# A two-layer mixture-of-experts kernel: head re-ordered, second gate moved to VectorE, five tiles brought home by one-hot products

## The chip, the cores and the metric

The kernel runs on one core of a Trainium2 chip, in one launch. The metric is the time of an execution on the device in microseconds (us). The engines are named as the profile names them: PE is TensorE, DVE is VectorE, ACT is ScalarE, POOL is GpSimd, and SP is SyncE, which here only issues transfers.

## The reference

The input x has 8 sequences of 256 rows (tokens) of 128 numbers, 2048 tokens in all. Two layers each add something to x. Everything is float32.

```python
# layer 0: conditioning by attention pooling, per sequence
scores = einsum('bsa,a->bs', tanh(x @ W1 + b1), v)
mask   = l <= j, l >= j or l != j, by the sequence's prompt type (0, 1, 2)
pooled = softmax(where(mask, scores, -1e30)) @ x / count(mask)
# layer 0: 8 experts, all computed, with gates from the logits
logits = pooled @ gate_weight.T
gates  = logits * (logits >= the 3072nd smallest of all 16384 logits)
x = x + sum_e gates[e] * (gelu_tanh(pooled @ w1[e].T + b1[e]) @ w2[e].T + b2[e])
# layer 1: an adapter chosen by the sequence's language, then a layer norm
h  = relu(x @ W1[lang] + b1[lang]) @ W2[lang] + b2[lang]
xc = layernorm(x + h) * gamma[lang] + beta[lang]
# layer 1: 8 experts, the two best per token
xn = layernorm(xc) * gamma + beta
w, idx = top_2(softmax(xn @ gate_w)), w normalised to sum 1
x = x + xc + sum over the 2 of w * (gelu(xn @ w1[e] + b1[e]) @ w2[e] + b2[e])
```

## The kernel before

The 2048 tokens are 16 blocks of 128, and these form four groups of four blocks. A list UNITS (L30) cuts the groups into five units: units 0 to 2 are whole groups of 512 tokens ("full units"), units 3 and 4 are halves of the last group with 256 tokens each.

**The head (L122 to L502)** runs as it is written, on PE, DVE, ACT and POOL. The tokens (xp, one tile per group) arrive on SP's and ACT's queues; all columns (col: weights with 32 or 8 columns, biases, gamma and beta) come by POOL's queue (L129), and after them the prompt types ptb (L130). Behind the tokens SP issues bva (the bias and v), the languages lgi, eight loads of the rows again in another layout (xg, L139), the sixteen loads of layer 0's weights (L144 and L147), and the loads that depend on the languages (L190 to L204). PE turns the tokens (turned_tokens, L238), forms the pooling's inner products (products, L247, "units" in the profile) and the gate's products (gate_logits, L260, "g0p"), both with columns of col; ACT takes the tanh (bent, L254); PE makes the scores (L281). DVE makes flags from the prompt types (own and out8, L312 to L318) and, in places (L321), the counts cnt of the tokens under the mask. Then come running maxima (scans, L347 and L349), their transposes by PE (tops, L365), the exponentials on ACT, and the pooling products with xg (L390).

**Layer 0's experts (layer, L895)** are PE's main work: for each unit and each expert four products hp_first (L945) and four yp_first (L925) of 512 columns, or of 256 in half units. ACT evicts hp_first with gelu (L947). DVE multiplies yp_first by a row of gates, gbc_first, and adds it up (accumulate, L901, with L913 and L915). SP loads gbc_first from DRAM into four buffers ahead of use (L905).

**Work beside it.** What else PE, DVE and POOL have to do in this stretch is written as generators. After each product call (in half units: after each second one) pump (L880) takes one step, up to the next `yield`, of the generator that stands first in the queue `behind`. So a number of yields between two steps is a number of product calls between two groups of PE instructions. PE's instructions have this order; a scheduler places those of the other engines. The first generators are the poolings of later groups and the threshold search (threshold, L521): DVE counts with an accumulating operation (L531) how many logits lie below trial values. When a unit's last expert is added up, its generator adapt (L689) is queued:

- It adds the tokens (L694), transposes the sum (fp, L566), projects down (adp, L704 to L707: one product for each of two sequences, 256 columns each, with two relu operations on DVE into ha) and up (dp, L711 to L716).
- The first layer norm (normed, L569: statistics on DVE, a power on POOL at L582, and a scaling by block at L587), gamma and beta of the language (L728 and L729), the second layer norm, whose result zr is also what is scattered.
- The second gate. After CHAIN_GAP = 5 yields PE transposes the normalised rows (znp, L749), DVE applies gamma and beta (znT, L754), PE multiplies by the gate's columns in four column groups (l1q, L763), DVE copies (l1s, L766), PE transposes back (l1p, L770), and DVE copies the logits (lg, L778). Half units use a shorter way without l1q (L775).
- DVE picks the two best experts (top_one, L597, twice) and forms running counts (sofar, L802). After two yields PE sums these over the tokens (kp, L808 and L809). From kp come the places in DRAM, and POOL scatters each block's rows, one indirect transfer per block and choice (L830), into xs, sorted by expert.
- After units 2, 3 and 4 (SLOTS, L32) DVE lists which tiles of 128 rows are complete (listed, L656).

**Layer 1's experts** work on 36 tiles of 128 rows (SURE, L46; three more behind a condition at L1184 are not needed with these inputs). Tile k is fetched with its weights by SP (L983 and L993), turned (xtp, L1019), and goes through hidden (hps, L1034, and gelu on ACT, L1036) and output (yps, L1043, and yt on DVE, L1047). hidden takes the expert's second bias from b2all (L1031), a copy of all eight rows on all partitions, loaded early (L629). POOL scatters the tile's rows yt into ys (L1050), two rows for each token. From tile PLACED = SURE − 4 = 32 on there is no scatter: DVE makes a 0/1 matrix by token (home, L1089), and PE multiplies it with yt (brought, L1103, "late" at L1106).

**The ending (L1160 to L1191)** runs as it is written on all engines. SP loads the two rows of each token back in eight pieces (yg; n counts sequences): n = 0 to FIRST − 1 after the scatter of tile 28, FIRST to 5 after that of tile 30 (L1055 to L1060), 6 and 7 at the start of the ending (L1164). DVE adds them (add, L1074: two operations), SP stores. For n = 6 and 7 the sums of late are added as well (L1182) and stored last. Of the four groups of late products, one stands before the last yps and three behind it.

## Time and profile before

| What | us |
|---|---|
| Median of 4 runs | 346.49 (345.98 to 347.41) |
| Profiled execution, its own time | 346.3 |
| Span of the profiled execution | 344.6 |
| Busy: PE | 335.5 |
| Busy: DVE | 197.3 |
| Busy: ACT | 170.6 |
| Busy: POOL | 93.5 |
| First hp_first (L945) starts at | 23.4 |
| First xtp (L1019) starts at | 260.5 |
| Last yps (L1043) starts at | 335.8 |

The profile shows one execution from its first to its last instruction, and its times count from the start of that span. The mean granted clock of PE was 0.998. A line of a timeline begins with a start and a duration in us and names the engine, the line of the kernel, the operation, what it writes and reads, and how many instructions it sums up; in brackets stands how long its engine was idle before it and what ended that. PE's instructions overlap, so that their cost is read from one start to the next. A product in float32 shows as two instructions. Groups give the busy time, the mean duration in ns, and the idle time before them.

### The profile page before, as it was taken

The numbers are of one execution on the slowest core, as the hardware profiler recorded it, in microseconds if no ns is written. First come the engines' busy times: TensorE is split into PE (matmuls) and PEld (weight loads), VectorE is DVE, ScalarE is ACT, GpSimd is POOL, SyncE is SP. The second block draws the span as 40 slices with busy tenths as digits, with TensorE's granted clock in tenths as the row PEclk, the third lists the DMA queues.
The fourth block names the chain that finished last, engine by engine and source line by source line (L and its number), as shares of the span: only waits on it lengthen the run. The fifth ranks groups of instructions, "written<-read, shape, count | busy, mean of one in ns | idle before, by whom it ended". The sixth has DMA issues, their size and how long they took to land. (4 is left out here: it accounts for less than half of the span.)

```text
span 344.6 us, 6117 instructions
## 1 busy us (share of the span) xinstructions
PE 335.5 (97%) x1662; PEld 221.2 (64%) x1662; DVE 197.3 (57%) x835; ACT 170.6 (50%) x393; POOL 93.5 (27%) x146
## 2 busy tenths in 40 slices
PE   7999999999999999999999999999999999999994
PEld 6795444444444444444444468877887999999993
DVE  2884766642235584757361247569768668733474
ACT  3476345543444333323543334644456777777660
POOL 6600000000000031174017001206604465765530
PEclk9999999999999999999999999999999999999999
DMA  6893599955214300121212010112376675587565
GB/s 179 252 342 74 143 345 384 380 191 145 76 56 141 80 30 30 30 86 39 62 38 62 23 30 30 42 35 73 81 204 166 169 205 171 156 218 217 147 208 178
DMA packets 35771, 47.56 MB, mean 138 GB/s; under 512 B 5449, under 2 KB 18588, under 8 KB 35736
## 3 DMA queue, kind: packets, MB, share of 16 engines
q1 hardware_dynamic: 32744, 42.17, 41.1%
q0 software_dynamic: 2144, 4.19, 3.6%
q10 hardware_dynamic: 848, 0.79, 0.7%
q8 instruction: 15, 0.25, 0.3%
q14 instruction: 20, 0.16, 0.2%
HBM read 32.66 MB, written 14.66 MB: 137 GB/s over the span
## 5 line engine op out<-in xcount | busy, mean ns | idle before, releaser
L947 ACT ACTIVATE hT_first<-hp_first,col 128x512 f32<-128x512 f32 (+1 forms) x160 | 93.2, 601 | 91.5 <-PE hp_first L945 90.4
L925 PE MATMUL yp_first<-hT_first,w 128*128 128x512 f32 (+1 forms) x320 | 120.1, 512 | 0.0
L945 PE MATMUL hp_first<-poolT,w 128*128 128x512 f32 (+1 forms) x320 | 119.8, 512 | 0.0
L925 PEld LDWEIGHTS yp_first<-hT_first,w 128*128 128x128 f32 x320 | 58.6, 190 | 45.3 <-issue 41.0
L945 PEld LDWEIGHTS hp_first<-poolT,w 128*128 128x128 f32 x320 | 58.7, 190 | 44.5 <-issue 39.7
L830 POOL DMA_INDIRECT xs<-zr,pos x32 | 32.5, 1015 | 67.6 <-DVE holding L653 33.0
L1036 ACT ACTIVATE hs<-hps,col 128x128 f32<-128x128 f32 x144 | 40.7, 375 | 11.8 <-PE hps L1034 8.3
L913 DVE SCALAR_TENSOR_TENSOR part_first<-yp_first,col,gbc_first 128x512 f32<-128x512 f32 (+1 forms) x28 | 17.2, 615 | 39.6 <-PE yp_first L925 39.1
L1043 PE MATMUL yps<-w,hs 128*128 x288 | 38.3, 277 | 0.5 <-issue 0.2
L1050 POOL DMA_INDIRECT ys<-yt,xt x32 | 31.9, 996 | 24.5 <-DVE yt L1047 14.9
L1034 PE MATMUL hps<-xc,wt 128*128 128x128 f32 x288 | 38.2, 276 | 0.0
L1043 PEld LDWEIGHTS yps<-w,hs 128*128 128x128 f32 x288 | 35.0, 192 | 1.1 <-issue 0.9
L1034 PEld LDWEIGHTS hps<-xc,wt 128*128 128x128 f32 x288 | 35.1, 192 | 0.4 <-issue 0.2
L582 POOL TENSOR_TENSOR rstd_l<-ve_l,nhalf 128x4 f32<-128x4 f32 (+1 forms) x5 | 5.0, 1005 | 69.4 <-DVE ve_l L580 69.3
L1047 DVE SCALAR_TENSOR_TENSOR yt<-yps,xt,b 128x128 f32<-128x128 f32 x36 | 12.5, 348 | 18.1 <-PE yps L1043 18.0
L915 DVE TENSOR_TENSOR acc_first<-acc_first,part_first 128x512 f32<-128x512 f32 (+1 forms) x35 | 20.1, 580 | 0.5
L1021 ACT ACTIVATE xc<-xtp,col 128x128 f32<-128x128 f32 x36 | 16.7, 470 | 7.1 <-PE xtp L1019 7.0
L516 POOL DMA_DIRECT2D gd_L<-gT_L x1 | 0.7, 660 | 61.1 <-DVE gT_L L514 61.1
L933 ACT ACTIVATE y_first<-yp_first,col 128x512 f32<-128x512 f32 x8 | 5.5, 687 | 23.2 <-PE yp_first L925 14.6
L1031 DVE TENSOR_TENSOR b<-b2all,xt 128x128 f32<-128x128 f32 x36 | 10.4, 289 | 8.0 <-DVE yt L1047 3.8
L531 DVE TENSOR_SCALAR_CACHE_REDUCE fl<-logit,tr 128x128 bf16<-128x128 f32 x46 | 13.5, 343 | 0.6
L550 DVE TENSOR_SCALAR_CACHE_REDUCE ok<-kt 128x3 f32<-128x3 f32 (+1 forms) x16 | 2.6, 160 | 13.8 <-PE kt L534 13.8
(253 smaller groups left out, 301.4 us busy)
## 6 DMA issues: line engine op xcount, KB each, us to landing
wt<-in_w_dram SPq DMA_DIRECT2D x36, 256.0 KB
xs<-empty SPq DMA_DIRECT2D x1, 8580.0 KB
w<-in_w_dram SPq DMA_DIRECT2D x24, 256.0 KB
gbc_first<-gd_L SPq DMA_DIRECT2D x24, 256.0 KB
xt<-xs SPq DMA_DIRECT2D x36, 65.0 KB
gbc_first<-gd_L SPq DMA_DIRECT2D x16, 128.0 KB
yg<-ys SPq DMA_DIRECT2D x8, 256.0 KB
xg<-in_x_dram SPq DMA_DIRECT2D x8, 128.0 KB
```

Source lines behind the costliest of these rows:

```text
L531: nc.vector.tensor_scalar(flags, lflat, values[:, i:i + 1], None, ALU.is_lt, ALU.add, accum_out=c[:, i:i + 1])
L830: move = nc.gpsimd.indirect_dma_start(out=xs, out_offset=bass.IndirectOffsetOnAxis(ap=pos[:, t:t + 1], axis=0), in_=zr[s][:, t, :], in_off ...
L913: nc.vector.scalar_tensor_tensor(part, y, bias, gbc, ALU.add, ALU.mult)
L915: nc.vector.tensor_tensor(accs[u], accs[u], part, ALU.add)
L925: nc.tensor.matmul(yp, lhsT=w2s[e][:, c, :], rhs=hT[:, c, :], start=(c == 0), stop=(c == HC - 1))
L945: nc.tensor.matmul(hp, lhsT=w1s[e][:, c * P:(c + 1) * P], rhs=sources[g][:, o * P:o * P + n], start=True, stop=True)
L947: nc.scalar.activation(hT[:, c, :], hp, act, bias=col[:, cb1 + e * HC + c:cb1 + e * HC + c + 1])
L1021: nc.scalar.activation(xc, tp, AF.Identity, bias=col[:, C_LB:C_LB + 1], scale=col[:, C_LG:C_LG + 1])
L1034: nc.tensor.matmul(hp[:, c, :], lhsT=wt[:, c * P:(c + 1) * P], rhs=xc, start=True, stop=True)
L1036: nc.scalar.activation(hT[:, c, :], hp[:, c, :], AF.Gelu, bias=b1all[:, bass.ds(number(k, ACT), 1), c])
L1043: nc.tensor.matmul(yp, lhsT=hT[:, c, :], rhs=w21[:, bass.ds(ek, 1), c * D:(c + 1) * D], start=(c == 0), stop=(c == HC - 1))
L1050: move = nc.gpsimd.indirect_dma_start(out=ys, out_offset=bass.IndirectOffsetOnAxis(ap=xt.bitcast(I32)[:, D:D + 1], axis=0), in_=yt, in_off ...
```

## The change

**Head.** The first 64 columns are loaded once more, as a tile of their own (near), by the third transfer on SP; the inner products and the gate's products of layer 0 use near. ptb is issued on POOL ahead of col. SP follows the written order in the head as well. The loads of the rows xg, of layer 0's weights and by language are now issued behind turned_tokens(3), and the first waits for its last transposes (further_loads). bva's product and the first tanh come before the third group's transposes. The flags own and out8 and the counts cnt are made by 16 operations on POOL instead of 14 on DVE, both calls of places ahead of the score products slp.

**Second gate of full units.** The transposes znp, znT, l1q, l1s and l1p are gone there. Once, a step second_gate forms the gate's columns times gamma, and their product with beta, as eight rows of 129 (g1p, two products), writes them to DRAM and loads them on all partitions. In each full unit 32 operations on DVE (8 experts, 4 blocks) multiply the normalised rows with such a row and sum up, with a yield after each third one, and one operation adds the beta part. Two more yields stand ahead of kp in full units. b2all now uses the same memory as the gate's rows and is loaded after unit 2's logits.

**Down-projection of full units.** Four products of 128 columns in four column groups, and four relu operations; for these the bias is copied by two small operations to the partitions of the other two groups. dp goes through the second sequence first.

**Last tiles.** PLACED is SURE − 5: tile 31 is brought home by products, too, and is not scattered. FIRST is 3. Two of five groups of late products stand before the last yps, and one more of the adds. The buffers of all eight yg are taken at once.

```diff
+    nc.gpsimd.dma_start(out=ptb, in_=ptype.partition_broadcast(P))
     nc.gpsimd.dma_start(out=col, in_=cols)
-    nc.gpsimd.dma_start(out=ptb, in_=ptype.partition_broadcast(P))
+    near = const.tile([P, 2 * A], F32, name="near")
     for g in range(NG - 1):
         for i, queue in enumerate((nc.sync, nc.scalar)):
+            if g == 2 and not i:
+                nc.sync.dma_start(out=near, in_=cols[:, :2 * A])
...
+    def further_loads(behind):
+        for g in range(NG):
+            for i in range(2):
+                move = nc.sync.dma_start(out=xg[g][:, 2 * i:2 * i + 2, :D], in_=xv[g, i])
+                tc.add_manual_dep(move.ins, behind.ins.name, SYNC, reason="the turned tokens come first")
...
     bent(0)
-    turned_tokens(3)
+    turned_tokens(2)
+    further_loads(turned_tokens(3))
...
-    for i, flag in enumerate((e0, e1)):
-        own = small.tile([P, B], F32, tag="own", name=f"own{i}", bufs=2)
-        nc.vector.tensor_tensor(own, flag, at_home, ALU.mult)
-        nc.vector.tensor_reduce(out8[:, i:i + 1], own, AX.X, ALU.add)
-    nc.vector.tensor_tensor(out8[:, 2:3], out8[:, 0:1], out8[:, 1:2], ALU.add)
+    own = const.tile([P, 2, B], F32, name="own")
+    nc.gpsimd.tensor_tensor(own, flags, at_home.unsqueeze(1).to_broadcast([P, 2, B]), ALU.mult)
+    for n in (4, 2):
+        nc.gpsimd.tensor_tensor(own[:, :, :n], own[:, :, :n], own[:, :, n:2 * n], ALU.add)
+    nc.gpsimd.tensor_tensor(out8[:, :2], own[:, :, 0], own[:, :, 1], ALU.add)
...
+    def second_gate():
+        scale = work.tile([P, P], F32, tag="gT", name="scale")
+        nc.vector.tensor_scalar(scale, ident, col[:, C_LG:C_LG + 1], None, ALU.mult)
+        yield
+        yield
+        g1p = pss.tile([E, D + 1], F32, tag="sm", name="g1p")
+        nc.tensor.matmul(g1p[:, :D], lhsT=col[:, C_G1:C_G1 + E], rhs=scale, start=True, stop=True)
+        nc.tensor.matmul(g1p[:, D:], lhsT=col[:, C_G1:C_G1 + E], rhs=col[:, C_LB:C_LB + 1], start=True, stop=True)
+        g1r = const.tile([E, D + 1], F32, name="g1r")
+        nc.vector.tensor_copy(g1r, g1p)
+        nc.sync.dma_start(out=g1d, in_=g1r)
+        eight("g1", g1d, D + 1)
...
+        if nt == GT:
+            for q in range(GT):
+                nc.tensor.matmul(hp[q * A:(q + 1) * A, :P], lhsT=lws[halves(u)[q // 2]], rhs=x2T[:, q * P:(q + 1) * P],
+                                 start=True, stop=True)
...
+        if nt == GT:
+
+            g1 = eights["g1"]
+            for n, (e, t) in enumerate(itertools.product(range(E), range(nt))):
+                spent = small.tile([P, D], F32, tag="spent", name=f"spent{u}_{n}", bufs=2)
+                nc.vector.scalar_tensor_tensor(spent, zn[:, t, :], 1.0, g1[:, e, :D], ALU.mult, ALU.mult,
+                                               accum_out=lg[:, t, e:e + 1])
+                if n % 3 == 2:
+                    yield
+            nc.vector.tensor_tensor(lg, lg, g1[:, :, D].unsqueeze(1).to_broadcast([P, nt, E]), ALU.add)
+            if u == NU - 3:
+                eight("b2", b2d, D)
             yield
...
+        if nt == GT:
+            yield
+            yield
         kp = pss.tile([P, GT + 1, E], F32, tag="sm", name=f"kp{u}")[:, :nt + 1, :]
...
-PLACED = SURE - 4
+PLACED = SURE - 5
...
     placed.append(output(*hid.popleft()))
-    brought(*placed[0], late, True)
-    store(nc.sync, *add())
+    for k in range(SURE - PLACED - 3):
+        brought(*placed[k], late, not k)
+    for _ in range(2):
+        store(nc.sync, *add())
     placed.append(output(*hid.popleft()))
-    for k in range(1, SURE - PLACED):
+    for k in range(SURE - PLACED - 3, SURE - PLACED):
         brought(*placed[k], late, False, LATE * (k == SURE - PLACED - 1))
-    for _ in range(FIRST, EARLY):
+    for _ in range(5, EARLY):
         store(nc.sync, *add())
```

## The prediction

> **What bounds the kernel now.** I read the shares of the engines first, then the slices of the span, the waits of TensorE (PE), and its timeline around one unit.

> ```profile
> PE 335.5 (97%) x1662; PEld 221.2 (64%) x1662; DVE 197.3 (57%) x835; ACT 170.6 (50%) x393; POOL 93.5 (27%) x146
> ...
> PE   7999999999999999999999999999999999999994
> ```

> PE is at work in 97% of the span, and in the slices only the first and the last are not full. So between those two, an instruction taken from PE shortens the program by its own time, and work on DVE (57%) costs nothing until PE waits for it. The waits say where it does:

> ```profile
> PE units L251 <- DMA col<-in_cols_dram: 1.1, 1, 1.1
> PE kp L808 <- DVE sofar L802: 0.7, 2, 0.3
> ```

> Columns: total, times, longest. Then PE's timeline (start, duration, instructions) through the second gate of unit 0:

> ```profile
> 133.03 2.74 PE L925 MATMUL yp_first<-hT_first,w 128*128 128x512 f32 x6
> 135.60 0.60 PE L749 MATMUL znp<-ident,zr 128*128 128x128 f32 x4
> 136.04 1.02 PE L925 MATMUL yp_first<-hT_first,w 128*128 128x512 f32 x2
> 136.90 1.02 PE L945 MATMUL hp_first<-poolT,w 128*128 128x512 f32 x2
> 137.85 0.43 PE L763 MATMUL l1q<-znT,col 128*32 128x128 f32 x8
> 138.21 1.98 PE L945 MATMUL hp_first<-poolT,w 128*128 128x512 f32 x4
> 140.03 0.27 PE L770 MATMUL l1p<-ident,l1s 128*128 128x128 f32 x1
> 140.14 1.02 PE L945 MATMUL hp_first<-poolT,w 128*128 128x512 f32 x2
> 141.00 2.74 PE L925 MATMUL yp_first<-hT_first,w 128*128 128x512 f32 x6
> 144.08 0.19 PE L808 MATMUL kp<-sofar,one 128*128 128x40 bf16 x1 [0.34 <-DVE sofar L802]
> ```

> Durations overlap, so I go by starts. Six instructions, three calls of 512 columns, take 135.60 − 133.03 = 2.57: **0.857 a call**. From 141.00 three calls would end at 143.57; kp starts at 144.08, so PE stood 0.51 for DVE.

> **Second gate (units 0 to 2).** Removed from PE, per unit: znp 0.44 (135.60 to 136.04); l1q 0.36 and another 0.09, by which the hp call before it lasts over 0.857; l1p 0.11 and 0.10 likewise (138.21 to 140.03 holds two calls, 1.71). That is 1.10, times three −3.3. The two g1p products come once; nothing is like them but l1p (0.11 to 0.21 each): +0.3.

> DVE gets 32 multiplications with a running sum per unit, 128x128. Their price d decides the change. Three rows stand near it:

> ```profile
> 41.11 0.35 DVE L531 TENSOR_SCALAR_CACHE_REDUCE fl<-logit,tr 128x128 bf16<-128x128 f32 x1
> 41.38 0.09 DVE L531 DVE_READ_ACCUMULATOR fl<-logit,tr 128x1 bf16 x1
> 41.38 0.34 DVE L531 TENSOR_SCALAR_CACHE_REDUCE fl<-logit,tr 128x128 bf16<-128x128 f32 x1
> ```

> ```profile
> L557 DVE SCALAR_TENSOR_TENSOR gate<-logit,found 128x128 f32<-128x128 f32 x1 | 0.4, 351 | 0.0
> ```

> The search's op has the same size and the same read of the accumulator, from one source; the next one starts 0.27 later, the 0.09 of the read inside. L557 is the new op's own kind, two SBUF sources in f32, without the accumulator: 351 ns, like L531's 0.35. So I take **d = 0.27**. Bounds: 0.20 below (L1031, a product of two SBUF tiles 128x128, lasts 289 ns, 0.06 less), 0.44 above (0.35 and 0.09 end to end).

> [...]

> Now the chain on DVE against PE. Unit 0's last normalised block ends at 131.5. With 32 × 0.27 = 8.6, the add (0.22), the accumulation in between as now (L913 and L915, 0.67 and 0.6), another L913 (0.67), and some 3.7 to 4 from the logits to sofar (140.34 to 144.02 today), sofar is ready near 146.4. On PE, kp stands 4 calls later in the stream (131 calls before it, then 135): 144.08 − 0.51 − 1.10 + 4 × 0.857 = 145.9. So kp waits 0.5, as today. Unit 1: DVE (normalised at 163.0) is ready near 177.9; kp moves 8 calls on, to 176.19 − 0.51 − 1.10 + 6.86 = 181.4: no wait, and today's 0.51 goes. Unit 2 (218.93, accumulations of half width): ready near 233.5, PE there at 232.36 − 0.23 − 1.10 + 6 × 0.43 = 233.6 (6 half calls on): today's 0.23 goes. So 0.5 is left of 1.25: I count −0.7.

> What is late next: DVE keeps a backlog after unit 2. Unit 3's dp waits for ha, which DVE reaches near 243.1 where PE wants it near 241.4; dp comes 89 half calls into that stretch instead of 80. Between 0 and 1.8; I take **+1.0**. On SP the broadcast of the gate's rows (528 KB) and, behind unit 2's logits, that of b2all (512 KB, the same tile) are issued. The second waits for DVE, and behind it SP holds the gates' rows gbc and the fetches of tiles; gbc goes three blocks (some 10 us) ahead, the first fetch is issued at 246.97 for a transpose at 260.54, and b2all is first read near 260. Hidden; without that cover it is 2 to 3 us. ha's two small copies and the scale hide under PE.

> **Down-projection.** adp goes from 0.56 (117.79 to 118.35, two products of 256) to four of 128 in four column groups, the form of l1q with 0.36 to 0.45. −0.15 three times: −0.45. Its outputs are taken by four DVE ops 32x128 instead of two of 32x256, inside the same two calls.

> **Head.** Units wait for the columns, from POOL's queue, until 6.76:

> ```profile
> 6.76 0.43 PE L251 MATMUL units<-xT,col 128*32 128x128 f32 x8 [1.07 <-DMA col<-in_cols_dram]
> ...
> 11.49 0.68 DVE L347 TENSOR_TENSOR_SCAN front<-scp,out 128x255 f32<-128x255 f32 x1
> ```

> A third transfer on SP brings the 64 needed columns near 5, and the eight loads of rows, which run on SP from 3.94 beside the tokens, stand behind the last transposes. Transposes 2 (7.29, waiting 0.37 for their tokens) then start near 6.2 to 6.4, and the scores (10.01 to 11.10 today) end near 10.0. The scan starts 0.4 after them today, since DVE makes the flags and a place table until 11.58; with these on GpSimd (16 small ops, 0.19 to 0.26 as L177 to L185) it starts when flags and scores are there, near 10.1: −1.35. PE's own work behind the scores (products, transposes, 2.7 us) lets tops start at 12.7 for 13.89. I take **−1.2**, bounds −1.6 and 0. The later row loads end near 11, the first weights near 14; the pooling needs rows at 16.16 and weights at 23.3, so both stay covered. If POOL is late with the flags, the scan waits for it instead: inside the same bounds.

> **Tail.** Five placed tiles mean four more one-hot products ahead of the last yps: 0.89, as today's four (334.87 to 335.76).

> ```profile
> 336.86 0.35 DVE L1047 SCALAR_TENSOR_TENSOR yt<-yps,xt,b 128x128 f32<-128x128 f32 x1 [0.65 <-PE yps L1043]
> ...
> 340.30 0.75 DVE L1182 TENSOR_TENSOR resid<-late,resid 128x256 f32<-128x256 f32 x2
> ```

> yt comes at 337.75 instead of 336.86; three pairs of adds (0.79 each: 337.13 to 337.92) instead of four follow, so L1182 comes at 0.89 − 0.79 = +0.1. Twelve products behind yps, as now, end at 340.4, just in front. **+0.15** (−0.2 to +0.9). The scatter of tile 31 leaves POOL; the adds there didn't wait for it, so I count nothing.

> **Sum.** Gate −3.3 + 0.3, kp −0.7, dp +1.0, adp −0.45, head −1.2, tail +0.15: −4.2. The profiled execution took 346.3 (span 344.6 and 1.7 around it), 0.2 under the median of the runs; 346.3 − 4.2 = 342.1, and against the median 342.3. I give **342.2**.

> **Rivals.**
> *DVE becomes the bound.* Each 0.01 of d moves sofar by 0.32 in units 0 and 2, where DVE and PE are level. The gain of 4.2 is used up when 64 × Δd reaches 4.2: d = 0.337; from there on it is slower. At 0.44 unit 0 waits 0.5 + 5.4, unit 1 1.9, unit 2 5.3: 12.6 more than counted, 354.7. Against it stand L531 and L557, for it that no row has both two sources and a sum. 0.17.
> *The head gives nothing and DVE's backlog more.* The tokens' transfers, not the rows', may set transposes 2, or the POOL flags the scan: +1.2. dp of unit 3 waits 1.8 and a little more: +1 to 2. 343.3 to 345.3, say 344.3. 0.21.
> *The covers hold.* No wait at dp (−1), none at kp (−0.5), the head 1.6: 340.2. 0.13.
> *It doesn't do what it says*: if the products stood in one block of 8.6 us on DVE, yp's results would wait, two buffers deep. In the order of the changed program they stand three by three between the accumulations, so I leave this with the first rival.

> **The numbers.** Forecast (341 to 343.3) 0.42, covers hold 0.13, second rival 0.21: faster by over 0.3% (1.0 us, about what a measurement of this kernel tells from no change) 0.76. DVE rival 0.17, slower. 0.07 for d near 0.33, within 0.3%. The range goes from 339.8 to 348.5: the first takes in nearly all of the third case, the second the unknown d up to 0.355; it leaves out the rest of the slow case, some 0.13, and 0.05 below. Faster cases alone: 339.8 to 345.3.

> **What would show it.** In the changed profile: the new op on DVE with starts 0.27 apart (right) or 0.40 (wrong); kp's waits in units 0, 1, 2 near 0.5, 0, 0; dp of unit 3 waiting up to 1.8 for ha; PE with fewer znp, l1q and l1p and 3.3 us less of them; units near 5.6, the scan near 10.1, tops near 12.7; L1182 0.1 later counted from the last yps of the tile before. I am wrong above all if DVE's sums are slower than one-source ops, or if the stream of PE calls before kp isn't as I counted it.

## The result: 0.4% slower

The changed kernel took 348.13 us (median of 51 runs, 346.12 to 351.47), the kernel before 346.46 (77 runs, 345.55 to 349.08). The ratio is 1.004, interval 1.003 to 1.005. The forecast was 342.2.

The profiled execution of the changed kernel is its fastest one: 346.12, span 344.4, mean clock of PE 0.988 where it was 0.998. On its page, the shares, PE's slices and the granted clock in the same slices (9 is 90% and more):

```profile
PE 332.8 (97%) x1647; PEld 222.8 (65%) x1647; DVE 216.0 (63%) x1024; ACT 170.4 (49%) x393; POOL 95.5 (28%) x161
...
PE   6999999999999999999999999999996999999993
...
PEclk9899999999999999999999999999998999999999
```

PE has 15 instructions fewer and is busy 2.7 us less, as the change meant. But slice 31 (from 258 us) has a hole that wasn't there, and in slices 2 and 31 the clock is below full. PE's waits (total, times, longest) name both places:

```profile
PE fp L567 <- DVE cf L664: 2.1, 1, 2.1
PE units L221 <- DMA near<-in_cols_dram: 1.4, 1, 1.4
...
PE bvp L292 <- DMA bva<-in_b1v_dram: 0.4, 1, 0.4
```

The wait of kp for sofar, which headed the list of before, is gone. Set beside the trace of before at the same instruction of the program, so at equal work of PE, the changed kernel is 1.0 late at the first pooled transposes (27.87 for 26.87), 0.3 ahead when unit 1's sum is transposed, 2.2 ahead at unit 2's, 3.7 at unit 3's, and **4.33 ahead** at the first hidden products of layer 1 (258.49 for 262.82). Twelve us later (xtp, 270.22 for 271.40) 1.2 is left. So there are two losses: the head, and the start of layer 1.

**The start of layer 1.** Three views of the changed kernel there. SP's timeline:

```profile
246.57 0.34 SPq L1032 DMA_DIRECT2D xt<-xs  x1
...
257.50 0.33 SPq L1032 DMA_DIRECT2D xt<-xs  x1
257.93 0.38 SPq L944 DMA_DIRECT2D gbc_first<-gd_L  x1
```

DVE's timeline:

```profile
261.39 0.48 DVE L952 SCALAR_TENSOR_TENSOR part_first<-yp_first,col,gbc_first 128x256 f32<-128x256 f32 x1 [1.08 <-DMA gbc_first<-gd_L]
...
262.39 0.23 DVE L664 TENSOR_SCALAR cf<-cf 128x8 f32<-128x8 f32 x1
```

PE's timeline:

```profile
258.49 1.95 PE L1073 MATMUL hps<-xc,wt 128*128 128x128 f32 x16
...
262.62 0.41 PE L567 MATMUL fp<-ident,acc_first 128*128 128x128 f32 x2 [2.08 <-DVE cf L664]
...
264.51 2.08 PE L1073 MATMUL hps<-xc,wt 128*128 128x128 f32 x8
```

The last row of gates (unit 4, expert 7) stands behind eight tiles' rows and seven tiles' weights, counted from the first tile's rows at 246.57; that is some 1.5 us a tile. DVE needs it for the last addition, and fp transposes that sum. Then eight hidden products take 2.08 where sixteen took 1.95: the granted clock, 1.00 from 260 to 264, is 0.57 from 264 to 268. The chain of waits gives the row's transfer as its longest piece:

```profile
257.93 3.37 DMA gbc_first<-gd_L
```

In the kernel before, lines of SP's timeline, of the operations that use such rows (with the first and the last start) and of PE's timeline:

```profile
258.69 0.38 SPq L905 DMA_DIRECT2D gbc_first<-gd_L  x1
...
L913 DVE SCALAR_TENSOR_TENSOR part_first<-yp_first,col,gbc_first x4: 472/482/484, 253.5 to 263.9; 128x256 f32<-128x256 f32 x4
...
262.82 1.95 PE L1034 MATMUL hps<-xc,wt 128*128 128x128 f32 x16
...
265.00 0.41 PE L566 MATMUL fp<-ident,acc_first 128*128 128x128 f32 x2
```

There the row was issued at 258.69, with seven tiles ahead of it, and used at 263.9. If its transfer took 3.37 there too, it had some 1.8 us to spare; that is an estimate, since DVE didn't wait and the landing doesn't show. PE's gain there is 4.3, the row's 0.76: the first tile's rows come after unit 2's eight scatters on POOL, which began only 0.9 earlier (233.34 for 234.24), and the changed program puts one more tile ahead of the row, 1.5 us.

**The tail** came as worked out: −1.18 at 270.22 and −1.28 at the last sum (L1229 at 339.02, for 340.30) leave nothing for it. But the span is only 0.2 shorter: the last store, issued at 339.80 for 341.08, ends the span 4.6 later, where it was 3.5. That isn't the new order of the tail: e9_tail below has the old one and takes 4.6, too. In two profiles of the kernel before it is 3.5 and 3.8, in those of the changed program 3.9 to 4.9. What these 1.1 us come from stays open.

The span's balance against before is so: +1.0 in the head, −5.3 in the units, +3.15 at the start of layer 1, −0.1 in the tail, +1.1 at the end, together −0.2. The median lies 2.0 above this profiled execution, where before it lies only 0.2 above: the changed kernel's executions had mean clocks of 0.981 to 0.993, those of before about 0.997.

### The profile page after: what moved, and what is told of

It reads as the page before. It is cut to its first block, busy times and chain, and to the rows that moved or that the text cites. A ratio compares the mean times of both kernels' runs of the same rounds, so it can differ in the third digit from the quotient of the medians.

```text
span 344.4 us, 6285 instructions
## 1 busy us (share of the span) xinstructions
PE 332.8 (97%) x1647; PEld 222.8 (65%) x1647; DVE 216.0 (63%) x1024; ACT 170.4 (49%) x393; POOL 95.5 (28%) x161
## 5 line engine op out<-in xcount | busy, mean ns | idle before, releaser
L964 PE MATMUL yp_first<-hT_first,w 128*128 128x512 f32 (+1 forms) x320 | 118.7, 511 | 0.0
L964 PEld LDWEIGHTS yp_first<-hT_first,w 128*128 128x128 f32 x320 | 59.4, 190 | 46.9 <-issue 41.7
L1073 PE MATMUL hps<-xc,wt 128*128 128x128 f32 x288 | 38.9, 280 | 0.0
L1089 POOL DMA_INDIRECT ys<-yt,xt x31 | 30.5, 983 | 24.9 <-DVE yt L1086 7.9
L1073 PEld LDWEIGHTS hps<-xc,wt 128*128 128x128 f32 x288 | 35.8, 196 | 0.4 <-DMA xt<-xs 0.3
L952 DVE SCALAR_TENSOR_TENSOR part_first<-yp_first,col,gbc_first 128x512 f32<-128x512 f32 (+1 forms) x28 | 17.2, 613 | 27.9 <-PE yp_first L964 26.4
L790 DVE SCALAR_TENSOR_TENSOR spent<-zr,g1all 128x128 f32<-128x128 f32 x96 | 21.2, 284 | 0.0
```

Source lines behind the costliest of these rows:

```text
L790: nc.vector.scalar_tensor_tensor(spent, zn[:, t, :], 1.0, g1[:, e, :D], ALU.mult, ALU.mult, accum_out=lg[:, t, e:e + 1])
L952: nc.vector.scalar_tensor_tensor(part, y, bias, gbc, ALU.add, ALU.mult)
L964: nc.tensor.matmul(yp, lhsT=w2s[e][:, c, :], rhs=hT[:, c, :], start=(c == 0), stop=(c == HC - 1))
L1073: nc.tensor.matmul(hp[:, c, :], lhsT=wt[:, c * P:(c + 1) * P], rhs=xc, start=True, stop=True)
L1089: move = nc.gpsimd.indirect_dma_start(out=ys, out_offset=bass.IndirectOffsetOnAxis(ap=xt.bitcast(I32)[:, D:D + 1], axis=0), in_=yt, in_off ...
```

## The experiments

**Theory A**: the gate's saving is real and is lost at the start of layer 1, since the row of gates hangs on SP's queue and not on PE. **Theory B**: the loss is the head's, and the gate on DVE saves little at the end. The runs stand in four groups (the expectations say "call"). Runs of one group share a chip and the runs of before; before took 354.15, 352.57, 354.34 and 346.58 in them, so between groups only ratios are compared. Even a ratio moves from group to group: the same kernel gave 0.9965 and 0.9923 (e1_gbc, e1_again), another 0.9929 and 0.9858 (e3_both, e3_again). So a difference of less than some 0.7% between two groups shows nothing. One visible difference: between 296 and 313 us PE stands 1.1, 1.7 and 1.7 in before_again and 3.5 to 3.6 in after_again, e6_gate and e7_join, and nowhere in the profiles of the fourth group and of the result; why is open.

| Run | What it is | Ratio to before | Interval |
|---|---|---|---|
| e1_gbc | row of gates early | 0.9965 | 0.9941 to 0.9989 |
| e2_head | head of before | 0.9977 | 0.9950 to 1.0004 |
| e3_both | both | 0.9929 | 0.9901 to 0.9957 |
| e4_fill | products in the head's waits | 1.0168 | 1.0125 to 1.0210 |
| after_again | changed kernel | 1.0059 | 1.0038 to 1.0081 |
| e5_fill | as e4, stores kept in place | 1.0063 | 1.0030 to 1.0095 |
| e6_gate | second gate on PE | 1.0036 | 1.0001 to 1.0070 |
| e7_join | products in the wait of fp | 0.9995 | 0.9975 to 1.0016 |
| e8_near | e1, columns first in the queue | 0.9955 | 0.9931 to 0.9979 |
| e9_tail | tail of before | 1.0072 | 1.0044 to 1.0101 |
| e10_idle | e3, products where fp waited | 0.9978 | 0.9950 to 1.0006 |
| after_third | changed kernel | 1.0045 | 1.0030 to 1.0061 |
| e1_again | row of gates early | 0.9923 | 0.9898 to 0.9948 |
| e11_gate_early | row early, second gate on PE | 0.9999 | 0.9984 to 1.0014 |
| e3_again | row early, head of before | 0.9858 | 0.9840 to 0.9875 |

**First group.** e1_gbc issues the last row behind two tiles:

```diff
+            rows_of[u, e] = gbc
+            return nc.sync.dma_start(out=gbc, in_=gates[0][...].partition_broadcast(P))
...
+            if (u, e) not in rows_of:
+                gates_row(u, e)
+            gbc = rows_of.pop((u, e))
...
+        tc.keep_in_program_order(gates_row(*due[0][:2]))
```

> The changed kernel, with the last gates row of layer 0 (unit 4, expert 7) issued by SP behind two of the eight first tile fetches instead of behind all eight. Theory A (the gain of the second gate is there until 258.5, 4.3 us ahead of before, and is lost because this row lands at 261.3, when PE has nothing left but work that waits for it; the idle 2.1 us also halve the granted clock for the next 4 us): the wait of fp for the last sum goes, the clock stays at 1.00 between 264 and 268, and the time falls by 3 to 4 us against the changed kernel, to 344 to 345. Rival B (the start of layer 1 is bound by the tiles' rows, scattered after unit 2's counts, not by this row): PE waits for xt or the lists instead, and the time falls by less than 1 us.

The wait of fp went, the clock stayed at 1.00 from 260 to 290 us, and the time is below that of before.

e2_head takes the head of before (columns from POOL, loads of rows beside the tokens, flags on DVE); e3_both takes both edits.

```diff
-    beginning.enter_context(tc.manual_schedule(engines={PE, DVE, ACT, POOL, SP}))
+    beginning.enter_context(tc.manual_schedule(engines={PE, DVE, ACT, POOL}))
...
-                nc.sync.dma_start(out=near, in_=cols[:, :2 * A])
...
-            nc.tensor.matmul(units[g][t * A:(t + 1) * A, :], lhsT=near[:, C_W1:C_W1 + A],
+            nc.tensor.matmul(units[g][t * A:(t + 1) * A, :], lhsT=col[:, C_W1:C_W1 + A],
```

> The changed kernel with the head of before (columns in one load on GpSimd's queue, flags on VectorE, rows and weights loaded early), the other three parts as changed. Theory A (the new head costs time: units start as late as before, b1 and v come later, and PE's idle halves the clock from 8.5 to 11.5): the pooling products start 1.0 us earlier, the clock stays at 1.00 in the head, and the time falls by 1 to 2 us, to 346 to 347. Rival C (a later start of layer 0 is covered by the wait at the end of layer 0, which the tile fetches set): less than 0.5 us.

> Both edits together: the head of before, and the last gates row issued behind two fetches. Theory A: the two losses add up, 4 to 6 us less than the changed kernel, 342 to 344, faster than before by 3 to 4. Rival B: no better than the head's edit alone by more than 1 us.

No changed kernel ran on this chip. Against the 1.004 of the result, the row gives 0.75% (2.6 us, 3 to 4 expected), the head 0.6%, both 1.1% (3.8 us, 4 to 6 expected). That each loss is there by itself and that they add up is so far only likely, as these steps hardly exceed what a ratio moves between groups; the fourth group has them on one chip.

e4_fill puts four products that nobody reads into the head's waits, to keep PE busy:

```diff
+    pass_time(3, ident, xp[1][:, 0, :])
...
+    pass_time(1, ident, xp[1][:, 0, :])
```

> The changed kernel with four products of 256 columns, whose result nobody uses, on PE: three while it waits for the near columns, one while it waits for b1 and v. Theory A (the idle time itself halves the clock in the head): units start at the same time or up to 0.1 later, the clock between 8 and 12 is 1.00, the pooling products start 1 to 1.5 us earlier, and the time falls by 1 to 1.5 us against the changed kernel. Rival D (the clock falls for another reason, such as the mix of work there): the clock stays near 0.5 from 9 to 11 and nothing is gained, or 0.1 to 0.4 lost.

A miss: in this build two stores of zeros came ahead of the loads of the rows on SP, and the pooling waited for them (1.9 us). The eight transposes behind the products did take 1.09 where e1_gbc's took 1.97.

**Second group.** The changed kernel again, e5_fill (e4 with the stores in their written place), e6_gate and e7_join. e6 puts the second gate back on PE (znp to l1p as in the code of before, with b2all loaded early), e7 puts six products that nobody reads between layer 1's first hidden products and the last sum's transposes:

```diff
-            for n, (e, t) in enumerate(itertools.product(range(E), range(nt))):
-                spent = small.tile([P, D], F32, tag="spent", name=f"spent{u}_{n}", bufs=2)
...
+                nc.tensor.matmul(lq[t * A:(t + 1) * A, :], lhsT=col[:, C_G1:C_G1 + A], rhs=zt[:, t * P:(t + 1) * P],
...
+    spare = psy.tile([P, GN], F32, tag="y", name="spare")
+    for _ in range(6):
+        tc.keep_in_program_order(
+            nc.tensor.matmul(spare[:, :2 * P], lhsT=ident, rhs=w21[:, 0, :2 * P], start=True, stop=True))
```

> The changed kernel as it is, for its time and profile beside the other runs of this call. Both theories: 0.3 to 0.5% slower than before, in its trace the wait of fp for the last sum at the end of layer 0.

> The changed kernel with four products of 256 columns on PE whose result nobody uses, three while PE waits for the near columns and one while it waits for b1 and v, and with the two stores that clear the last rows of ys held in their written place, behind the loads of the rows. Theory A (idle time slows PE down): transposes 2 and 3 take 1.1 us instead of 1.5 to 2.0, the pooling products start 0.5 to 1.5 us earlier than in the changed kernel beside it, and the time falls by as much. Rival D (PE is slow there for another reason): the transposes take as long as before the edit, and the time is the same or up to 0.5 us more.

> The changed kernel with the second gate of full units on PE again, as before the change (four transposes, four products, one transpose back, no broadcast of gate rows, two yields less ahead of kp), everything else as changed. Theory A (what the gate saves on PE, some 5 us by the trace, is lost at the end of layer 0 and in the lists behind it): no more than 2 us slower than the changed kernel; fp of the last unit no longer waits 2 us. Rival E (the gate's saving reaches the end, and the loss is elsewhere, in the head): 3.5 to 5 us slower than the changed kernel.

> The changed kernel with six products of 256 columns whose result nobody uses, 1.3 us at full clock, put on PE between the first two hidden products of layer 1 and the transposes of the last sum, where PE waits. Theory A (PE idles for 2.1 us and then runs slow for some 4 us): the transposes start no later, PE behind them is at full clock, and the time falls by up to 1.5 us. Rival: the slow stretch is not from idle time, and the time is the same, or up to 0.6 us more.

The changed kernel repeats its result; there the head kept its pace, and fp waited 3.2. e5_fill says nothing: its products overran the waits by 1.1, the poolings began 1.2 later, and the total is the same. e6_gate is the sharpest of these: with 1.1 us more on PE in each of three units the kernel is no slower than the changed one (353.43 for 354.62). e7_join is faster than the changed kernel, by 0.6% with intervals that don't touch, for work that serves nothing. Its PE timeline:

```profile
261.84 2.75 PE L1188 MATMUL spare<-w,ident 128*128 128x256 f32 x12
...
264.66 0.41 PE L567 MATMUL fp<-ident,acc_first 128*128 128x128 f32 x2
...
266.97 1.16 PE L1073 MATMUL hps<-xc,wt 128*128 128x128 f32 x8
```

The dummies fill the time in which PE stood, and the hidden products behind them take 1.16 at a granted clock of 1.00 (256 to 272), where after_again's take 2.08 at 0.50 (264 to 268). The dummies take 2.75, where the expectation put 1.3, and PE still waits 1.3 behind them. So the time after the wait is lost to the clock, beside the wait itself.

**Third group.** The kernel before in one profile; e8_near (e1, with near first on SP and bva first on ACT's queue); e9_tail (changed kernel with PLACED = SURE − 4, FIRST = 4 and the old order of adds); e10_idle (e3 with four such products where e7 has six).

```diff
+    nc.scalar.dma_start(out=bva, in_=b1v)
+    nc.sync.dma_start(out=near, in_=cols[:, :2 * A])
     for g in range(NG - 1):
...
-FIRST = 3
+FIRST = 4
...
-PLACED = SURE - 5
+PLACED = SURE - 4
```

> The kernel before as it is, for its profile on the chip of this call. All theories: no wait of fp for the last sum at the end of layer 0, the last gates row lands before it is used, and PE's clock is whole there.

> The changed kernel with the last gates row behind two fetches (as in the first run of this kind), and the head's small loads first: the near columns are SP's first transfer, b1 and v are ACT's first. Theory A (the new head gains nothing because near, third on SP, lands at 6.7 as the whole columns did before, and b1 and v later): units start near 5.6 instead of 6.7, bvp without a wait, the pooling products 0.8 to 1.3 us earlier than the changed kernel's 16.0 to 17.2, and the time 0.5 to 1.3 us below that of the gates row's edit alone, which stood at 0.9965 of before. Rival C (the head isn't bound by these two): units still wait for near or the tokens until 6.5 or later, and nothing is gained.

> The changed kernel with four placed tiles, the loads and the order of the ending as before, everything else as changed. By the prediction (0.15 us) and by theory A: within 0.7 us of the changed kernel, which stands at 1.004 to 1.006 of before, so 1.002 to 1.008. Rival (the five placed tiles cost the 0.9 us that their products take): 1.001 to 1.003.

> The head of before, the last gates row behind two fetches, and four products of 256 columns whose result nobody uses between the first hidden products of layer 1 and the last sum's transposes. Theory A (what is left of PE's idle time there, some 2.5 us in the run with both edits, still slows PE): 0.5 to 1.5 us below that run, which stood at 0.993 of before. Rival: the idle time there is too short to slow PE, and the four products cost what they take, 0 to 0.9 us.

before_again (353.57) shows no wait of fp and a clock of 1.00 from 260 to 300. In e8_near the units start at 6.05 and bvp at 6.40 without waiting; but the transposes wait for the tokens, 0.29 ahead of the units and 0.55 behind them, and the tops start at 13.58, for 13.71 in e1_again below. So there the tokens set the head's end; that the whole is no faster than e1 compares two chips. e9_tail at 1.0072 stands beside the 1.004 to 1.006 of other chips: the new tail is worth nothing or a little. e10_idle missed, and it shows no price of the products either. 0.9978 stands beside the 0.9929 of another chip, and in its profile PE stands 2.6 behind the products for DVE, which itself stood for something that the profile doesn't name, and the next eight hidden products take 2.08 (granted clock 0.64 from 264 to 268). e2_head, e4_fill, e6_gate and e9_tail have such a wait, too (1.5 to 1.9), e3_both and e3_again have not.

**Fourth group.** Until here the early row and the gate on PE stood on different chips. Here three corners of the square stand on one chip, with e3 beside them; the fourth corner, e6_gate, is from the second group. e11_gate_early is e6 with e1's edit; two of its lines:

```diff
+        tc.keep_in_program_order(gates_row(*due[0][:2]))
...
-                nc.vector.scalar_tensor_tensor(spent, zn[:, t, :], 1.0, g1[:, e, :D], ALU.mult, ALU.mult,
-                                               accum_out=lg[:, t, e:e + 1])
```

> The changed kernel as it is, on the chip of the next three. Theory A (the gate's saving is lost at the start of layer 1, because the last row of gates is issued behind eight tile fetches): a ratio to the kernel before of 1.004 to 1.006, with a wait of 2 to 3 us on fp. Theory B (the gate's saving was never there; the loss comes from the head and the rest): the same ratio, so this run alone tells nothing; it is the corner of a square of four.

> Second corner: the changed kernel with the last row of gates issued behind two fetches. Theory A: 0.7 to 1.0% (2.5 to 3.5 us) faster than the changed kernel of this call. Theory B: within 0.3% of it.

> The corner that was missing: the second gate back on PE as before the change, and the last row of gates issued behind two fetches. With the row late, the gate on PE was 0.2% faster than the changed kernel. Theory A: with the row early the order is turned round, the gate on PE is 0.7 to 1.1% (2.5 to 4 us) slower than on DVE (the second corner), and no faster than the changed kernel by more than 0.3%. Theory B: gate on PE and gate on DVE stay within 0.3% of each other here too.

> The best version so far once more (row early, head as before the change). It was at 0.993 of the kernel before. Both theories: 0.992 to 0.995; 0.3 to 0.5% below the second corner, which is the head's price beside its rival on the same chip. If the two are within 0.1%, the head's price was a matter of the chip.

| Second gate on | Row late | Row early |
|---|---|---|
| PE | 1.0036 (1.0001 to 1.0070), e6 | 0.9999 (0.9984 to 1.0014), e11 |
| DVE | 1.0045 (1.0030 to 1.0061), after_third | 0.9923 (0.9898 to 0.9948), e1_again |

With the row early the gate on DVE is 3.2 us faster than on PE (343.56 and 346.74); with the row late it gained nothing (354.62 and 353.43 on the chip of the second group). The early row is worth 4.3 us with the gate on DVE (347.87 and 343.56). Theory A holds, more strongly than I expected, and theory B's second half falls. Its first half stands: the head of before is another 2.0 us faster (341.57), more than the 0.3 to 0.5% expected. e3_again, **0.9858**, beats both kernels.

In e1_again the row is issued behind two tiles, and PE doesn't wait for it. SP's timeline:

```profile
248.31 0.38 SPq L947 DMA_DIRECT2D gbc_first<-gd_L  x1
```

and PE's:

```profile
259.24 0.38 PE L567 MATMUL fp<-ident,acc_first 128*128 128x128 f32 x2
260.54 0.49 PE L1092 MATMUL yps<-w,hs 128*128 x2 [0.91 <-ACT hs L1085]
...
261.41 1.16 PE L1083 MATMUL hps<-xc,wt 128*128 128x128 f32 x8
```

From the profiles of the changed kernel and e1_again: the first hidden products of layer 1 start 1.1 apart (258.49 and 257.35, nearly all of it from the head), those after dp 4.6 apart (268.33 and 263.70), the last yps 4.3 (335.28 and 331.00). So 3.5 us go at this junction: some 1.8 by standing (2.08 and 0.59, where e1_again stands 0.91), some 0.9 by the eight products at 2.08 for 1.16, the rest by the products behind them.

## Why the prediction was wrong

**The gate on PE: right.** Each unit is 1.1 ahead by it; the two g1p products cost 0.53 for 0.3.

**The price d on DVE: the right row, on the safe side.** DVE's timeline of the changed kernel:

```profile
133.12 0.28 DVE L790 SCALAR_TENSOR_TENSOR spent<-zr,g1all 128x128 f32<-128x128 f32 x1
133.33 0.08 DVE L790 DVE_READ_ACCUMULATOR spent<-zr,g1all 128x1 f32 x1
133.33 0.28 DVE L790 SCALAR_TENSOR_TENSOR spent<-zr,g1all 128x128 f32<-128x128 f32 x1
```

Starts are 0.21 apart (0.27 predicted, bounds 0.20 to 0.44), and the read of the accumulator costs nothing beside the next one (both start at 133.33). No run shows the 0.40 that the prediction sets as the sign of a miss: the new operation, with two sources in f32 and a running sum, starts every 0.21, where the search's, with one source, starts every 0.27 in the kernel before. So kp waits nowhere in units 0 to 2 (−1.25 instead of −0.7), dp of unit 3 doesn't wait (0 instead of +1.0), and the rival "DVE becomes the bound" fell.

**Down-projection: right**, −0.2 a unit for −0.15.

Together these were −3.15 in the sum and came to −5.3 by the start of layer 1 (from 1.0 late to 4.33 ahead). The terms named make 4.6 of it; 0.7 I can't place, and it arises between unit 3's sum (3.7 ahead) and the first hidden products (4.33).

**The step that failed: SP "hidden".** The prediction costed the new transfers on SP at nothing because "gbc goes three blocks (some 10 us) ahead". That holds where rows alone are issued. The last row, in the kernel before, was issued 5.2 ahead of its use (258.69 for 263.9). It is issued among the fetches of tiles, and its time is set by the chain of unit 2's scatters on POOL and SP's 1.5 us a tile. I asked whether the change makes that chain later, and it doesn't; I didn't ask what happens when PE comes earlier than it. The view of before had the answer, as an estimate: 1.8 us to spare, plus the 0.8 that the row itself moved, caps what can pass the end of layer 0 at 2.6 us. What comes above that turns into standing (2.08 at fp), and here the granted clock fell with it (0.50 from 264.33 to 267.74): 3.15 of the 4.33 were gone at 270.22, where the sum had put nothing. One row moved ahead brings 4.3 us on one chip. No rival named this. The second rival allowed for a head that gives nothing (+1.2), and that half came true, in part for the reason it named (the tokens, in e8_near).

**The head: wrong sign.** −1.2 was expected, with units near 5.6 and the scan near 10.1. The flags on POOL were in time, and the scan starts when the scores end, but the scores ended no earlier. near, third on SP, was issued at 1.75 and used at 6.77, just when col had come from POOL in the kernel before (6.76). Behind it bva, moved ahead of the third group's transposes and issued at 3.42, held PE again:

```profile
6.77 0.43 PE L221 MATMUL units<-xT,near 128*32 128x128 f32 x8 [1.36 <-DMA near<-in_cols_dram]
7.64 0.24 PE L292 MATMUL bvp<-bva,ident 32*32 32x2 f32 x8 [0.44 <-DMA bva<-in_b1v_dram]
7.81 1.50 PE L210 MATMUL xTp<-ident,xp 128*128 128x128 f32 x8
```

Even where near comes early, bva takes the time back; e1_again's PE:

```profile
5.89 0.42 PE L221 MATMUL units<-xT,near 128*32 128x128 f32 x8
7.45 0.24 PE L292 MATMUL bvp<-bva,ident 32*32 32x2 f32 x8 [1.13 <-DMA bva<-in_b1v_dram]
7.62 1.09 PE L210 MATMUL xTp<-ident,xp 128*128 128x128 f32 x8
```

There the tops start at 13.71, for 13.90 before. In the changed kernel's own profile they start at 14.90, and the reason is the pace: the eight transposes take 1.50 for 1.09, at a granted clock of 0.58 in 8 to 10 us. Of the nine profiles with the changed head (products in the waits and e8_near left out) six ran these transposes slowly (1.50 or 1.97) and had their tops at 14.9 to 16.4, three at 1.09 with tops at 13.4 to 13.8. Of the six with the head of before one did (e3_both, two groups of four at 1.12 for 0.66, tops at 14.62), the others' tops were at 13.0 to 14.0. The six are of two kinds. In the changed kernel, after_third and e6_gate PE had come to full pace (units in 0.43) and fell back at 8.33, 7.40 and 7.56. In e1_gbc, e7_join and e9_tail it had not come up yet (units in 0.65 to 0.66), and did so only at 10.6, 14.1 and 10.6; e3_both is such a case, too. So the head gains next to nothing at its best, and loses 1 to 2.5 us where PE runs at half pace behind its waits, which it does more often than before. That cost of a wait was in no step.

On one chip the head of before is worth 2.0 us (e1_again and e3_again), but the profiled execution of e1_again, with tops at 13.71 and a clock of 1.000, is among its fastest (342.12; 342.11 to 345.03). Its others had mean clocks of 0.990 to 0.995, those of e3_again 0.996 to 1.000. That fits a loss by pace in executions that no trace shows; it isn't shown directly. Which piece of the head costs (the columns, the order of the loads, the flags) no run tells apart.

**The tail: right**, 0 for +0.15.

## What to carry to other kernels

Before costing a saving on the engine that bounds, look downstream for the first transfer or buffer that doesn't hang on that engine, and read how long before its use it lands: that slack caps the saving. A small transfer that is needed soon belongs ahead of a train of big ones on its queue; here one row moved gave 1.2%, more than the whole change was meant to. And ask of a load that is moved forward what the engine waits for next, in order, since the next wait takes the gain.

## What the runs showed of the hardware

**PE's granted clock, as the 18 traces record it.** Columns: stretch, its length, busy time of PE, PEld, DVE, ACT and POOL, then PE's granted clock, the share of the DMA engines, and GB/s; the changed kernel:

```profile
260.00:264.00 4.00, 1.34 (x10) 0.86 (x9) 2.92 (x13) 2.91 (x10) 2.69 (x3) 1.00 0.83 227
264.00:268.00 4.00, 4.00 (x23) 3.40 (x21) 2.08 (x14) 1.60 (x5) 0.00 (x0) 0.57 0.18 36
268.00:272.00 4.00, 4.00 (x36) 3.88 (x37) 2.88 (x20) 2.24 (x8) 1.23 (x2) 1.00 0.53 163
```

| Run | Stretch | PE busy, of 3.41 | Clock in it | Clock behind it |
|---|---|---|---|---|
| changed kernel | 4.92 to 8.33 | 1.61 | full | half |
| changed kernel | 260.92 to 264.33 | 1.12 | full | half |
| after_again | 258.74 to 262.15 | 0.69 | full | half |
| e6_gate | 4.15 to 7.56 | 1.57 | full | half |
| after_third | 3.98 to 7.40 | 1.59 | full | half |
| after_third | 259.98 to 263.39 | 2.09 | full | full |
| e7_join | 263.23 to 266.64 | 2.11 | full | full |
| after_again | 262.15 to 265.56 | 2.62 | half | half |
| after_again | 265.56 to 268.98 | 3.41 | half | full |

In the 18 traces together (the last 8 us of an execution left out) the clock fell behind 22 stretches at full clock, in which PE was busy 0.2 to 1.77 us; in the changed kernel's, these are its two least busy ones (1.12 and 1.61; the next has 3.0). It fell behind none of some 1700 with more, and behind five with 1.5 to 1.77 it didn't fall either. From half clock it rose behind stretches busy 3.14 us or more, and stayed behind those of 1.98 to 3.02; the first stretches of an execution are left out of this. So the length of a wait alone doesn't tell: in after_third PE waited 1.77 us twice, for near and at fp, and the clock fell behind the first alone (busy 1.59 and 2.09 of 3.41 in the two stretches). Where the stretches begin differs from one execution to the next (4.92, 4.15 and 3.98 in the three heads of the table).

In these traces the granted clock doesn't always show the pace: in e1_gbc, e7_join and e9_tail it stands at 1.00 in 8 to 12 us while the transposes take 1.97 for 1.09. The records of the clock begin there only at the first change (10.6, 14.1, 10.6), so the durations are the better witness.

**A transfer of 32 KB third in a queue** was used without a wait at 5.7 and 5.9 us in two executions (e11_gate_early, e1_again), and waited for until 6.6 to 7.0 in the seven others of the same head, issued at 1.75 each time.
